# Later sums, a deeper staging ring and an even chain pattern in a transformer block

## The chip, the core and the metric

The kernel runs on one core of a Trainium2 chip. The metric is the device time of one execution in microseconds. Before the change it is 2608.06 us, the median of three runs (2605.62 to 2611.5).

A core has a matrix engine (PE, with its weight loads shown as PEld), a vector engine (DVE), a scalar engine (ACT), GpSimd (POOL) and SyncE (SP). Each runs its instructions strictly in the order in which they were put, and waits where an operand or a buffer is not ready. Here SP only issues DMAs; ACT and POOL issue some too, in their own order of work.

## The reference

```python
x = x + attention(tc_rmsnorm(x, t, g1, b1), Wq, Wk, Wv, Wo)
x = x + swiglu(tc_rmsnorm(x, t, g2, b2), gate_w, hid_w, out_w)
# around it: out = x_in + x
# tc_rmsnorm: g * x * rsqrt(mean(x * x) + 1e-6) + b, with g and b linear in t
# attention:  16 heads of 32, softmax(q k^T / sqrt(32)) v, then Wo
# swiglu:     silu(x @ gate_w.T) * (x @ hid_w.T) @ out_w.T, hidden width 2048
# x: (4, 1024, 512) float32; t: (4, 128)
```

## The kernel before

The 4096 tokens are eight blocks of 512 (two to a batch entry). The heads are taken in groups of four. One **unit of attention** `j` is half a block's queries (256) for one head group; its 1024 keys come in four **slots** of 256 keys. So there are 8 x 4 x 2 x 4 = 256 slots `g`, 32 to a block, and a loop `while g < END` writes out by hand what each engine does in each slot. The order of the instructions on PE, DVE, ACT and POOL is exactly that of the code. SP's DMAs are ordered by the scheduler. `kind = g % 4` is the place of a slot in its **group** of four.

What a slot does:

- `scores(g)` multiplies queries and keys on PE into four PSUM banks (tag `sc`, one tile); `keep(g)` copies them on ACT to an SBUF tile `raw` (a ring of nine); `running_max` takes maxima on DVE, in two instructions.
- In kind 0 `max_T` transposes the maxima of the unit before on PE, `parts` reduces them on DVE, and in kind 1 `parts_T` and `spread` bring them back as `shift`, with copies on ACT.
- Five slots after `scores`, `shifted` subtracts the maximum (DVE) and `exponential` follows (ACT); six slots after, `weighted` multiplies by the values (PE), and `accumulate` adds the slots of one unit in SBUF with an accumulating DMA of 1 MB (POOL).
- The **sums of a unit**: `fold_sum` (DVE) adds the two halves of the accumulated tile, `sums` (PE) adds over partitions into a PSUM tile of tag `w` (two banks), `sums_out` copies it to SBUF (ACT) and writes it to DRAM; `take` reads it back in another layout, `invert` takes the reciprocal (DVE), `put` writes it, and `sums_in` spreads it over partitions; `normalize` applies it. `sums_out`, `take` and `put` issue their DMAs from ACT; `sums_in` from SP. For the last two units `inverse` takes the reciprocal directly.

Slots 0 to 59 are the **opening** (`FS` is 60). There PE also computes the projections of keys, queries and values for all four batch entries. One projection of 512 tokens is a **chain**: PE fills one bank, ACT evicts it (`evict`) to a staging tile of tag `st`, a ring of two, and SP stores it to DRAM (`kqs`, `vs`), from where the attention loads it later. The chains wait in a queue with the slot from which each may run. A credit decides how many run in a slot: it grows by `PACE` = 1.5 per slot, up to 2.9, and each chain that runs takes 1. The first chain of a slot is evicted in the same slot, the second (`late`) early in the next. Chains of the output projection (`project_out`) have their own queue, `first`; when one is `due` it goes ahead.

From slot 60 the **feed-forward** fills PE instead. A pair `p` of slots makes 128 hidden features for one block: `pair_15`, `pair_26`, `pair_7`, `pair_3` and `pair_4` are products that share sums of weights and tokens (tiles `pa` of tag `w`, and `pb`); `take_5`, `add_15`, `copy_156` and `sub_5` combine them on ACT and DVE; `gate_tanh`, `gate` and `hidden` make the feature tile `h` (a ring of seven), which frees `pa` and `pb`. `filler` contracts four finished features with `out_w` (tile `pc`, tag `w`). The kinds 0 and 2 are the even slots of a pair, 1 and 3 the odd ones. `take_5` also uses a tile of tag `st`.

In the profile the lines are: `mm` L106 (all 32-column products), `take` L152, `invert` L157, `put` L162, `spread_inverse` L168, evictions L235 and L248, `scores` L278, `keep` L285, `running_max` L290 and L293, `max_T` L299, `parts` L305 to L310, `parts_T` L315 and L317, `spread` L325 and L326, `shifted` L331, `exponential` L334, `weighted` L344, `accumulate` L358, `fold_sum` L366, `sums` L376, `sums_out` L381 with its DMA at L146, `take_5` L496, `add_15` L500, `copy_156` L515, `sub_5` L522, `gate` L537, `hidden` L540, `take_contract` L553.

Of the kernel before, what the change touches and what calls it, by code (L numbers as in the profile page):

```python
# [10 lines left out]
F32 = mybir.dt.float32  # L11
# [6 lines left out]
P = 128  # L18
NB = 512
# [5 lines left out]
def tile_cond_transformer_block(  # L25
# [133 lines left out]
    def put(tag: str):  # L159
        few = state.pop(("few", tag))  # L160
        inv_s[tag] = tc.dram_tile(list(few.shape), F32, name=f"invs{tag}")
        nc.scalar.dma_start(out=inv_s[tag], in_=few)  # L162
# [55 lines left out]
    def load_wkq(hg: int):  # L218
        t = sb.tile([P, 2, C, P], F32, tag="fw", name=f"wkq{hg}", bufs=4)
        nc.sync.dma_start(out=t, in_=kq_w[hg])  # L220
        wkq[hg] = t


    def project_kq(b: int, hg: int, which: int, half: int):
        pp = bank(f"pkq{b}_{hg}_{which}_{half}")
        for c in range(C):
            mm(pp, wkq[hg][:, which, c, :], y[b, half][:, c, :], c == 0, c == C - 1)

        def evict():
            if (b, hg) == (0, 0) and (which, half) != (1, 1):  # L230
                at = which * L + half * NB
                t = kq[0][:, at : at + NB]
            else:
                t = sb.tile([P, NB], F32, tag="st", name=f"st{b}_{hg}_{which}_{half}", bufs=2)
            nc.scalar.activation(t, pp, AF.Copy, scale=SCALE if which else 1.0)  # L235
            nc.sync.dma_start(out=kq_s[b, hg][:, which, half * NB : (half + 1) * NB], in_=t)

        return evict

    def project_v(b: int, kt: int):  # L240
        half, col = divmod(kt * P, NB)
        pp = bank(f"pv{b}_{kt}")
        for c in range(C):
            mm(pp, y[b, half][:, c, col : col + P], wv[0][:, c, :], c == 0, c == C - 1)

        def evict():
            t = sb.tile([P, NB], F32, tag="st", name=f"sv{b}_{kt}", bufs=2)
            nc.scalar.copy(t, pp)  # L248
            nc.sync.dma_start(out=v_s[b][:, :, kt, :], in_=t.rearrange("p (a c) -> p a c", a=C))

        return evict
# [15 lines left out]
    def scores(r: int):  # L267

        j, u = divmod(r, UN)
        m, qh = divmod(j, NB // HQ)  # L270
        t = kq[m]
        sc = ps_sc.tile([P, HG, 2, HQ], F32, tag="sc", name=f"sc{r}")
        q0 = L + qh * HQ
        for k in range(2):
            kt = 2 * u + k
            for i in range(HG):
                rows = slice(i * DH, (i + 1) * DH)
                nc.tensor.matmul(  # L278
                    sc[:, i, k, :], t[rows, kt * P : (kt + 1) * P], t[rows, q0 : q0 + HQ], start=True, stop=True
                )  # L280
        raw[r] = sb.tile([P, 2, HG, HQ], F32, tag="raw", name=f"raw{r}", bufs=RAW)
        state["sc", r] = sc

    def keep(r: int):
        nc.scalar.copy(raw[r].rearrange("p k h q -> p h k q"), state.pop(("sc", r)))  # L285

    def running_max(r: int, k: int):
# [76 lines left out]
    def fold_sum(j: int):  # L364
        t = acc[j]
        nc.vector.tensor_tensor(t[:, 0, :, :], t[:, 0, :, :], t[:, 1, :, :], ALU.add)  # L366
# [5 lines left out]
    def sums(j: int):  # L372
        total = ps.tile([P, HQ], F32, tag="w", name=f"sum{j}")
        a = acc.pop(j)
        for i in range(HG):
            nc.tensor.matmul(total[i * DH : (i + 1) * DH, :], ones_sum, a[:, 0, i, :], start=True, stop=True)  # L376
        state["sum", j] = total

    def sums_out(j: int):
        t = sb.tile([P, HQ], F32, tag="rec", name=f"total{j}", bufs=2)  # L380
        nc.scalar.copy(t, state.pop(("sum", j)))  # L381
        compact(f"s{j}", t, DH, HQ)
# [6 lines left out]
    def inverse(j: int):  # L389
        rec = sb.tile([P, HQ], F32, tag="rec", name=f"rec{j}", bufs=2)  # L390
        nc.vector.reciprocal(rec, state.pop(("sum", j)))  # L391
        state["rec", j] = rec
# [141 lines left out]
    def gate(p: int):  # L534

        h[p] = sb.tile([P, NB], F32, tag="h", name=f"h{p}", bufs=7)
        nc.vector.scalar_tensor_tensor(h[p], state.pop(("t", p)), 1.0, bank_a.pop(p), ALU.add, ALU.mult)  # L537
# [117 lines left out]
    def chain(g: int, spare: int = 0):  # L655

        q = first if first and first[0][0] <= g else queue
        if not q or (g >= 0 and q[0][0] > g) or (q is queue and len(q) <= spare):
            return None
        _, load, fn, a = q.popleft()  # L660
        if load is not None:
            fetch()
        return fn(*a)

    with tc.manual_schedule(
# [34 lines left out]

        direct = NR // UN - 2
        late = None
        credit = 0.0
        g = 0
        END = NR + 12
        NP_ = NBLK * NF
# [20 lines left out]
        while g < END:  # L727
# [19 lines left out]
                scores(g)  # L747
            if kind == 1 and m_on:
                spread(j_m, 0)
            if kind == 3 and s_on:  # L750
                fold_sum(j_s)
            if kind == 0 and n_on and j_n >= direct:
                inverse(j_n)
            if x_on and kind != 1:
                shifted(r_x)
            if late is not None:
# [5 lines left out]
                normalize(j_o)  # L762
            if kind == 1 and n_on and j_n < direct:
                take(f"s{j_n}")
            if kind == 3 and n_on and j_n < direct:
                put(f"s{j_n}")
            for fn, a in pinned.pop(g, []):
                fn(*a)
            if v_on:
# [6 lines left out]
                shifted(r_x, slice(HG // 2, HG))  # L776
            if g < NR:
                keep(g)
            if kind == 0 and o_on:
                sums_in(j_o)  # L780
            if kind == 1 and s_on:
# [2 lines left out]
            if not ffn:  # L784
                if x_on:
                    exponential(r_x)
                credit = min(credit + PACE, 2.9)
                evict = None
                if credit >= 1 or due or kind == 0:
                    evict = chain(g, FG)  # L790
                    credit -= evict is not None
                if g < NR:
                    running_max(g, 0)
                    running_max(g, 1)
                if evict is not None:
                    evict()
                for fn, a in halfway.pop(g, []):
                    fn(*a)
                if kind == 0 and m_on:
                    columns[0] = P  # L800
                    max_T(j_m)
                    parts(j_m)
                if g == FS - 1:
                    columns[0] = DH
                    pair_15(0)
                    take_5(0)
                    add_15(0)
                elif credit >= 1 or due or kind == 0:
                    late = chain(g, FG)
                    credit -= late is not None  # L810
                if kind == 3 and s_on:
                    sums(j_s)
                    sums_out(j_s)
                if g in (FS - 4, FS - 3):
                    load_f(0, g - FS + 4)
                if g == FS - 1:
                    load_f(1, 0)
            elif even:
                load_f(p + 1, 1)
                pair_26(p)  # L820
                copy_156(p)
                if x_on:
                    exponential(r_x)
                if kind == 0 and m_on:
                    max_T(j_m)
                    parts(j_m)
                one, two, evict = filler(p)
                one()
                two()
                if g < NR:  # L830
                    running_max(g, 0)
                    running_max(g, 1)
                if evict is not None:
                    evict()
                if kind == 0:
                    pair_7(p)
                    sub_5(p)
                for fn, a in halfway.pop(g, []):
                    fn(*a)
            else:  # L840
                load_f(p + 2, 0)
                if due or len(queue) > FG:
                    chain(g)()
                if kind == 3:
                    pair_7(p)
                    sub_5(p)
                pair_3(p)
                if kind == 3:
                    gate_tanh(p)
                if x_on:  # L850
                    exponential(r_x)
                pair_15(p + 1)
                take_5(p + 1)
                if kind == 1:
                    gate_tanh(p)
                if g < NR:
                    running_max(g, 0)
                if kind == 3:
                    gate(p)
                if g < NR:  # L860
                    running_max(g, 1)
                add_15(p + 1)
                if kind == 1:
                    gate(p)
                pair_4(p)
                hidden(p)
                if due:
                    chain(g)()
                if kind == 3 and s_on:
                    sums(j_s)  # L870
                    if j_s < direct:
                        sums_out(j_s)
                for fn, a in halfway.pop(g, []):
                    fn(*a)
            if kind == 2 and n_on and j_n < direct:
# [98 lines left out]
```

## Time and profile before

| what | value |
|---|---|
| median of three runs | 2608.06 us |
| the profiled execution, its own time | 2606.2 us |
| its span | 2604.4 us |
| PE busy | 2434.4 us, 93% of the span |
| DVE busy | 1845.1 us, 71% |
| ACT busy | 1409.4 us, 54% |
| moved by DMA | 510.64 MB, 196 GB/s on average |
| granted PE clock, mean | 0.98 |

A profile line for a group of instructions gives the source line, engine and operation, what is written and read with the shape, how often, the busy time, the mean of one, and the idle time of the engine just before it with what ended most of it. A line of the waits reads "engine, tile and line that waited <- what it waited for: microseconds in total, times, longest". A line of the timeline gives the start, the length, the instruction and, in brackets, how long the engine had been idle and what released it. "pa L106 x16" in a timeline is several instructions of the same kind merged; the start of the next line tells better than the length when the engine could go on, since lengths of matmuls overlap.

### The profile page before, as it was taken

What the parts mean: (1) busy time and instruction counts of PE and PEld (TensorE: products, weight loads), DVE (VectorE), ACT (ScalarE), POOL (GpSimd) and SP (SyncE); (2) the same over time, 40 slices, a digit from 0 to 9 for tenths busy, and PEclk for the clock granted to TensorE, in tenths of its full rate; (3) what the DMA queues carried; (4) which work ended last, traced back from release to release, by engine and by line L of the source; (5) the groups of instructions that cost most, each with busy time, mean ns of one, the idle gap of its engine ahead of it and who ended that gap; (6) DMA issues with size and microseconds to landing.
All of it is one profiled execution on the core that took longest, in us unless ns stands there. A gap on an engine that the chain in (4) does not pass through costs nothing. (4 is left out here: it accounts for less than half of the span.)

```text
span 2604.4 us, 71655 instructions
## 1 busy us (share of the span) xinstructions
PE 2434.4 (93%) x31785; PEld 1134.6 (44%) x31785; DVE 1845.1 (71%) x2180; ACT 1409.4 (54%) x1485; POOL 172.4 (7%) x207
## 2 busy tenths in 40 slices
PE   8899898899999899999999999999999999989999
PEld 3333333334444444444444444444444444434444
DVE  2677676857777888788868886887788778843332
ACT  3566666666556655665655665655566556512110
POOL 0000000000000000000000000000000000000000
PEclk9999999999999999999999999999999999999999
DMA  5698898877887888789878887888788878763442
GB/s 193 178 256 238 222 243 212 225 201 187 209 195 183 209 226 209 175 200 226 209 184 200 217 217 182 202 210 211 189 203 208 211 190 194 188 173 107 136 133 90
DMA packets 216386, 510.64 MB, mean 196 GB/s; under 512 B 43407, under 2 KB 84359, under 8 KB 188686
## 3 DMA queue, kind: packets, MB, share of 16 engines
q0 software_dynamic: 28656, 208.68, 41.5%
q1 hardware_dynamic: 166752, 296.56, 34.8%
q8 instruction: 250, 4.10, 0.6%
q10 hardware_dynamic: 20670, 0.83, 0.6%
q14 instruction: 58, 0.48, 0.1%
HBM read 254.82 MB, written 42.48 MB: 114 GB/s over the span
## 5 line engine op out<-in xcount | busy, mean ns | idle before, releaser
L331 DVE TENSOR_TENSOR raw<-raw,shift 128x2048 f32<-128x2048 f32 (+1 forms) x320 | 595.1, 1860 | 128.6 <-ACT shift L326 123.3
L285 ACT COPY raw<-sc 128x2048 f32<-128x2048 f32 x256 | 479.9, 1875 | 171.8 <-DVE fews L157 63.7
L334 ACT ACTIVATE raw<-raw 128x2048 f32<-128x2048 f32 x256 | 491.2, 1919 | 130.5 <-DVE raw L331 130.3
L290 DVE TENSOR_TENSOR rmax<-rmax,raw 128x1024 f32<-128x1024 f32 x384 | 469.5, 1223 | 67.1 <-ACT raw L285 61.9
L106 PE MATMUL pc<-h,ow 128*32 128x512 f32 x4096 | 468.7, 594 | 0.2 <-DVE rec L391 0.2
L106 PE MATMUL pa<-x,fw 128*32 128x256 f32 x6144 | 383.2, 382 | 6.8 <-DVE pa L500 6.8
L278 PE MATMUL sc<-kq 32*128 32x256 f32 x4096 | 302.3, 410 | 10.1 <-ACT raw L285 10.1
L344 PE MATMUL av<-raw,v 128*32 128x256 f32 x4096 | 282.2, 394 | 18.7 <-ACT raw L334 18.6
L358 POOL DMA_DIRECT2D raw<-raw x192 | 165.3, 861 | 2023.6 <-ACT raw L334 911.8
L106 PE MATMUL pa<-sums,fw 128*32 128x256 f32 x4096 | 269.2, 381 | 0.0
L106 PEld LDWEIGHTS pa<-x,fw 128*32 128x32 f32 x6144 | 194.6, 110 | 159.2 <-issue 24.6
L278 PEld LDWEIGHTS sc<-kq 32*128 32x128 f32 x4096 | 190.1, 189 | 145.8 <-issue 103.4
L106 PE MATMUL pkq<-y,wkq 128*32 128x512 f32 (+1 forms) x1760 | 237.4, 608 | 9.1 <-ACT y L182 4.1
L106 PEld LDWEIGHTS pc<-h,ow 128*32 128x32 f32 x4096 | 128.8, 110 | 244.0 <-issue 218.8
L344 PEld LDWEIGHTS av<-raw,v 128*32 128x32 f32 x4096 | 109.1, 111 | 147.3 <-issue 56.3
L106 PEld LDWEIGHTS pa<-sums,fw 128*32 128x32 f32 x4096 | 133.8, 111 | 88.9 <-issue 1.8
L106 PE MATMUL pb<-sums,fw 128*32 128x256 f32 x2048 | 137.7, 387 | 31.0 <-DVE pb L522 30.4
L305 DVE TENSOR_REDUCE top<-mt 128x8 f32<-128x1024 f32 x64 | 78.3, 1223 | 104.8 <-PE mt L299 104.8
L532 ACT ACTIVATE t<-pa 128x512 f32<-128x512 f32 x128 | 78.1, 610 | 111.9 <-PE pa L106 111.9
L553 DVE SCALAR_TENSOR_TENSOR res<-pc,res 128x512 f32<-128x512 f32 x128 | 88.2, 689 | 70.1 <-PE pc L106 70.1
L106 PE MATMUL pb<-x,fw 128*32 128x256 f32 x2048 | 134.0, 379 | 1.2 <-ACT pb L515 1.2
L106 PEld LDWEIGHTS pkq<-y,wkq 128*32 128x32 f32 (+1 forms) x1760 | 72.3, 118 | 143.6 <-issue 128.3
(100 smaller groups left out, 1894.8 us busy)
## 6 DMA issues: line engine op xcount, KB each, us to landing
raw<-raw POOLq DMA_DIRECT2D x192, 1024.0 KB, 8.8
fw<-sw SPq DMA_DIRECT2D x256, 256.0 KB
ow<-in_out_w SPq DMA_DIRECT2D x128, 256.0 KB
fw<-in_gh_w SPq DMA_DIRECT2D x128, 256.0 KB
wkq<-in_kq_w SPq DMA_DIRECT2D x32, 512.0 KB
v<-vs SPq DMA_DIRECT2D x32, 512.0 KB
fw<-in_gh_w SPq DMA_DIRECT2D x128, 128.0 KB
kq<-kqs SPq DMA_DIRECT2D x31, 512.0 KB
```

The lines of the kernel that those rows point to most:

```text
L106: nc.tensor.matmul(dst[k : k + n, :], w[:, k : k + n], moving, start=start, stop=stop, skip_group_check=seeded)
L278: nc.tensor.matmul(sc[:, i, k, :], t[rows, kt * P : (kt + 1) * P], t[rows, q0 : q0 + HQ], start=True, stop=True)
L285: nc.scalar.copy(raw[r].rearrange("p k h q -> p h k q"), state.pop(("sc", r)))
L290: nc.vector.tensor_tensor(rmax[j], rmax[j], raw[r][:, k, :, :], ALU.max)
L305: nc.vector.tensor_reduce(top, state.pop(("mt", j)), AX.X, ALU.max)
L331: nc.vector.tensor_tensor(t, t, s.unsqueeze(1).to_broadcast(list(t.shape)), ALU.add)
L334: nc.scalar.activation(raw[r], raw[r], AF.Exp)
L344: nc.tensor.matmul(av[j][i * DH : (i + 1) * DH, :], v[m][:, kt, i * DH : (i + 1) * DH], raw[r][:, k, i, :], start=(kt == 0), stop=(kt == K ...
L358: nc.gpsimd.dma_start(out=acc[j].rearrange("p k h q -> p (k h q)"), in_=raw[r].rearrange("p k h q -> p (k h q)"), accum_op=ALU.add,)
L532: nc.scalar.activation(state["t", p], bank_a[p], AF.Tanh, scale=0.5)
L553: nc.vector.scalar_tensor_tensor(r, pp, 0.5, r, ALU.mult, ALU.add)
```

## The change

Four edits:

1. In the opening, staging tiles come from the ring of `h` (seven tiles) instead of `st` (two), through a new helper `staging`. From the moment the sums of tokens exist (end of slot 58) they come from `st` again.
2. The fold of a unit moves from the head of its kind 3 slot to the end of it (opening), or to the place between `add_15` and `hidden` (feed-forward). `sums` moves from the end of that slot to the next slot, kind 0, right behind `scores`; `sums_out` follows `keep` there.
3. `put` moves behind `keep` in its slot, kind 3. The `raw` tile of a slot is allocated in `keep` instead of `scores`.
4. The credit goes. In the opening every slot runs one chain, and every even slot a second: two, one, two and one in a group.

```diff
+    def staging(name: str):
+        if "sums" in state:
+            return sb.tile([P, NB], F32, tag="st", name=name, bufs=2)
+        return sb.tile([P, NB], F32, tag="h", name=name, bufs=7)
...
-                t = sb.tile([P, NB], F32, tag="st", name=f"st{b}_{hg}_{which}_{half}", bufs=2)
+                t = staging(f"st{b}_{hg}_{which}_{half}")
...
-            t = sb.tile([P, NB], F32, tag="st", name=f"sv{b}_{kt}", bufs=2)
+            t = staging(f"sv{b}_{kt}")
...
-        raw[r] = sb.tile([P, 2, HG, HQ], F32, tag="raw", name=f"raw{r}", bufs=RAW)
         state["sc", r] = sc
     def keep(r: int):
+        raw[r] = sb.tile([P, 2, HG, HQ], F32, tag="raw", name=f"raw{r}", bufs=RAW)
...
             if kind == 1 and m_on:
                 spread(j_m, 0)
-            if kind == 3 and s_on:
-                fold_sum(j_s)
-            if kind == 0 and n_on and j_n >= direct:
-                inverse(j_n)
+            if kind == 0 and n_on:
+                sums(j_n)
+                if j_n >= direct:
+                    inverse(j_n)
...
-            if kind == 3 and n_on and j_n < direct:
-                put(f"s{j_n}")
...
             if g < NR:
                 keep(g)
+            if kind == 0 and n_on and j_n < direct:
+                sums_out(j_n)
+            if kind == 3 and n_on and j_n < direct:
+                put(f"s{j_n}")
...
-                credit = min(credit + PACE, 2.9)
-                evict = None
-                if credit >= 1 or due or kind == 0:
-                    evict = chain(g, FG)
-                    credit -= evict is not None
+                evict = chain(g, FG)
...
-                elif credit >= 1 or due or kind == 0:
+                elif even:
                     late = chain(g, FG)
-                    credit -= late is not None
                 if kind == 3 and s_on:
-                    sums(j_s)
-                    sums_out(j_s)
+                    fold_sum(j_s)
...
                 if kind == 1:
                     gate(p)
+                if kind == 3 and s_on:
+                    fold_sum(j_s)
                 pair_4(p)
                 hidden(p)
...
-                if kind == 3 and s_on:
-                    sums(j_s)
-                    if j_s < direct:
-                        sums_out(j_s)
```

## The prediction

> **What bounds the kernel now.** I read the page's busy table first, then the stretches by 100 us, then the waits of PE, ACT and DVE in two windows (opening 0 to 620 us, feed-forward 620 to 2380), then the timelines of single slots.
>
> ```profile
> PE 2434.4 (93%) x31785; PEld 1134.6 (44%) x31785; DVE 1845.1 (71%) x2180; ACT 1409.4 (54%) x1485; POOL 172.4 (7%) x207
> 300.00:400.00 100.00, 87.69 (x844) 33.40 (x843) 67.27 (x73) 61.91 (x65) 6.88 (x8) 0.92 0.85 239
> 700.00:800.00 100.00, 96.93 (x1346) 45.73 (x1342) 76.40 (x92) 53.98 (x56) 7.74 (x9) 1.00 0.81 194
> ```
>
> PE bounds, so what counts is PE's idle time and its slowed time. In the stretches (columns: length, then PE, PEld, DVE, ACT, POOL busy, clock, DMA share) the opening is the poor part: PE 88% busy at clock 0.92, against 97% at 1.00 later.
>
> ```profile
> ACT st L235 <- DMA kqs<-st: 46.3, 9, 8.4
> 345.17 0.60 ACT L235 ACTIVATE st<-pkq 128x512 f32<-128x512 f32 x1 [7.61 <-DMA kqs<-st]
> 347.46 0.58 PE L325 MATMUL sp<-mT,select 12*128 12x256 bf16 x2 [1.89 <-ACT mT L317]
> 347.97 1.94 PE L344 MATMUL av<-raw,v 128*32 128x256 f32 x16
> ```
>
> First line, ACT's waits in the opening: an eviction of a projection waits for the store of an earlier one, which holds one of two `st` buffers. The others show one case: ACT stands 7.61 us, the copy of `mT` behind it is late, PE idles 1.89 us, and then 16 matmuls that take 1.07 us elsewhere take 1.94, at a lower clock.
>
> ```profile
> PE sum L376 <- DVE h L537: 23.0, 38, 0.7
> PE pb L106 <- DVE pb L522: 30.4, 10, 4.8
> ACT raw L285 <- DVE fews L157: 61.2, 31, 2.0
> 994.16 1.05 PE L106 MATMUL pb<-sums,fw 128*32 128x256 f32 x16
> 995.79 0.64 PE L376 MATMUL sum<-raw,ones_sum 128*32 128x256 f32 x8 [0.58 <-DVE h L537]
> 996.36 1.15 PE L278 MATMUL sc<-kq 32*128 32x256 f32 x16
> 990.30 1.17 DVE L366 TENSOR_TENSOR raw<-raw 128x1024 f32<-128x1024 f32 x1
> 995.06 0.68 DVE L537 SCALAR_TENSOR_TENSOR h<-t,pa 128x512 f32<-128x512 f32 x1
> 995.66 1.22 DVE L290 TENSOR_TENSOR rmax<-rmax,raw 128x1024 f32<-128x1024 f32 x1
> 996.79 0.43 DVE L500 TENSOR_TENSOR pa<-pa,p 128x256 f32<-128x256 f32 x1
> ```
>
> These are waits in the feed-forward, then the end of a kind 3 slot. `sums` waits for a PSUM bank that `gate` (L537) frees. DVE has no gap in this slot, from the fold (L366) to the end: its order, not its load over the whole, sets the moment.
>
> **What the Trainium skill says.** "TensorE: Matmul & The Clock Gate", "What's actually happening": an idle array falls to half clock and needs a busy window of about 3.4 us to recover. The slowing agrees (1.94 against 1.07 us); the page's idle window of 3.4 us doesn't, waits of 2.3 us suffice here. "Perfetto Trace Analysis", "Optimization Strategy": a bubble that repeats can mean too few buffers. Agrees: nine waits on `st`. "DMA: Bandwidth & Descriptors", "Anatomy of one DMA — SWDGE (gpsimd) path": a semaphore wait ahead of a DMA is made by the issuing sequencer. Agrees: `keep` (L285) stands up to 2.0 us behind `put`, whose reciprocal is late.
>
> **The change, part by part.** Sums are against this execution: 2606.2 us, span 2604.4; the median of the runs shown, 2608.06, is 1.9 above.
>
> *Staging in the `h` ring (seven).* From PE's timeline, slot 0 starts at 49.7 us and slot 60 at 592.5. Eight groups of four slots, 186.0 to 477.7, take 36.46 each. PE's own work in one, by start to start: six chains of 3.55 (333.82 to 337.37), four scores 1.08, four weighted 0.89, sums 0.55, transposes 0.92, parts and spreads 0.85: 31.5. The excess of 5.0 is 3.1 idle (24.9 in the eight) and 1.5 of clock (windows of 20 us: 0.59 of a window lost). Of the 24.9, I trace to ACT stalls on stores: 1.89 at 347; 2.33 and 2.50 after 313.9; 2.61 and 0.66 after 392.8; 1.84 after 236.4; 0.91 after 244.6: 12.7. With 2.0 at 124 and 2.6 at 567 it is 17. Clock lost in the windows with such stalls is 0.77 of 20 us, 15; half of it, 8, I put to them, since DVE's waits lie there too. Together 25. Six chains come in 36 us, so seven buffers last about 40 us against a store's 7.4 (issued 337.80, released 345.17): no wait remains. Late next is `parts` on DVE, which keeps PE 2.33 us at five places whatever ACT does; I give back 4. **Gain 21.**
>
> *Two, one, two, one.* The credit gave 2,2,1,2 and 2,1,1,1 by turns; the chains are as many (four left at slot 60 both times), so PE's work is equal. With no second chain ahead of `sums`, a wait like the 4.16 us at 591.5 (bank held by the last eviction) goes, and ACT no longer holds `keep` for `total` (17.0 us in eight waits, mostly free). 9 us, bounds 0 and 15. Loads in SP's queue swap places with a few stores here; at a DMA share of 0.85 I count nothing, bounds of 5 either way. POOL's order is unchanged.
>
> *Fold and sums.* Nothing is removed. Normal group, with the case above: the fold leaves the slot's head, so `shifted`, `sub_5`, the maxima and `gate` end 1.1 earlier; the fold follows `add_15` and ends at 995.66 - 1.09 + (1.13 + 0.33 + 1.09) = 997.1. PE ends `pair_4` at 995.1, runs scores to 996.2, **waits 0.95 us for the fold**, sums to 997.75, where `weighted` starts; before it started at 997.44. With semaphores +0.4 us. `hidden` ends as before; behind PE's wait stand `weighted` and all of the next slot. Some 30 groups: +12. In six groups with two output projections in the slot, the wait of 0.81 for `x` goes: -5. In six with a norm, where sub_5 keeps PE 3.30 us and sums and scores run at half clock (2.1 and 1.0 us), `weighted` can start near 1143.1 instead of 1144.1: -6. In three, fold waits for a transfer (12.1 us in four waits, to 5.9) and pb loses 1.6 to 2.3; the fold now comes later: -6. The last two groups take their inverse in the slot of the sums: 1 us either way. **Net -5**, bounds -15 and +15. In the opening the fold behind the maxima costs 0 to 0.8 in 14 groups: +5.
>
> *Moved DMAs, all on ACT's queue.* `put` behind `keep`: 1.4 us later, and SP's first spread load with it (990.41 to 997.90 now, 7.5 us; SP waits there 94.1 us in all). Behind it on SP stand weight loads that are used over 13 us later, and the spread rows are used at 1017: nothing. `sums_out` behind `keep`: issued near 998.5 to 1000 instead of 996.9, while `take` reads it at 1007.3. The gap falls from 10.4 to 8 or 9. One landing shows indirectly: 1206.35 to 1207.90. So nothing; if it took as long as `put`'s 7.5 to 9, ACT and PE lose up to 0.8 in 48 groups. Raw tiles allocated in `keep` take the same buffers as built: nothing either way.
>
> Sum: -21 - 9 + 5 - 5 = -30: 2576 for the profiled execution, **2578** as a median.
>
> **Rivals.** *The next limit takes it (chance 0.14).* With ACT free, DMA (share 0.85 to 0.93 in the opening) and DVE's `parts` catch PE: staging gives 5, pattern 0, fold costs 5, feed-forward as above: about 2603. For it: 2.33 us waits on `parts` repeat. Against: 12.7 of 24.9 us of idle follow store stalls. *The stores still hold ACT* (the change doesn't do what it says) gives the same. *The fold becomes the bound (0.09), slower.* In kind 0, PE waits for a fold behind `add_15`, itself behind ACT's copy `p` and a 1.9 us exponential. At 0.4 us a normal group it costs 12; 1.0 us more, 1.4, eats the whole gain of 30, and 1.9 gives 2608 + 15 = 2623. For: DVE is dense there. Against: `p` is copied by 995.9, before `add_15` wants it. *Full floor*: the opening near 32.5 a group, 2550; inside the first forecast's tail.
>
> **Numbers.** Forecast 0.77. 0.2% is 5.2 us, about what a measurement of this kernel can tell: faster below 2602.8. Nearly all of the forecast (0.76) and half of the next-limit case (0.07) make 0.83; the other half is same, 0.07; the fold's case and a rest of 0.01 are slower, 0.10. The range 2555 to 2606 takes in opening gains from about 0 to 50 and leaves out the fold's case and the floor.
>
> **What would show it.** Right: no `st` wait on `kqs` above 1 us; slots 0 to 60 in about 518 us instead of 542.8; opening clock above 0.96; PE's wait at L376 <- DVE fold, about 1 us in 30 groups, in place of `h`; normal group 30.9 instead of 30.5 us; no `keep` behind `fews`. Wrong: ACT waiting at `take` for `sumss`; opening groups still over 35.5 us with DVE or DMA as releaser; fold waits over 1.4 us.

## The result and the profile after

The changed kernel takes **2618.15 us** (median of 12 runs, 2609.97 to 2625.4) against 2609.78 of the kernel before in the same session (12 runs): a ratio of **1.0031, 95% interval 1.0015 to 1.0047**. It is 8 us slower, where 30 faster was forecast. The profiled execution has a span of 2618.8 us and a time of 2620.56.

The stretches of the kernel after, columns as before (length, busy PE, PEld, DVE, ACT, POOL, clock, DMA share):

```profile
300.00:400.00 100.00, 94.94 (x950) 38.24 (x953) 77.09 (x83) 71.14 (x74) 7.67 (x9) 0.98 0.96 263
700.00:800.00 100.00, 96.91 (x1352) 47.12 (x1344) 78.06 (x91) 58.28 (x61) 7.75 (x9) 1.00 0.80 188
```

The stretch that was poor is mended: PE 95% busy at clock 0.98, where it had 88% at 0.92. The loss must lie elsewhere. From PE's timeline, by the starts of slots 0, 60 and 252:

| | slots 0 to 60 | slots 60 to 252 |
|---|---|---|
| before | 542.8 us | 1640.7 us |
| after | 527.2 (-15.6) | 1667.9 (+27.2) |

The waits of the kernel after, of ACT over the whole run and of PE in the feed-forward (total us, times, longest):

```profile
ACT shift L332 <- DMA rec<-invss: 39.9, 10, 5.0
ACT raw L291 <- DMA raw<-raw: 81.0, 35, 5.9
PE pa L106 <- ACT shift L332: 30.0, 11, 3.9
PE sum L382 <- issue: 27.9, 14, 7.5
PE sum L382 <- PE sc L284: 21.7, 23, 1.0
```

Lines 1 and 3 are new: in the kernel before no `shift` copy waits longer than 0.73 us for a DMA. ACT's copy of `shift` (L332) waits ten times for a DMA that has nothing to do with it, and PE behind it. Lines 4 and 5 are PE waiting at `sums`, in both for the fold, though the releaser named is another: in the trace the fold ends 0.1 us ahead of `sums` each time, and both lines are gone in the experiments that put the fold first. The second line stands where `keep` waited for `fews` before (63.7 us in the whole run, now 11.7): with `put` gone from ahead of it, `keep` waits longer for the accumulating DMA that frees its `raw` buffer (81.0 us against 46.6 before).

The timeline of the kernel after, group 100:

```profile
931.05 5.30 SPq L168 DMA_DIRECT2D rec<-invss  x4
...
938.35 0.58 ACT L332 COPY shift<-sp 128x512 f32<-128x512 f32 x1 [0.92 <-PE sp L331]
...
942.76 0.32 ACTq L152 DMA_DIRECT2D fews<-sumss  x1
...
943.13 0.58 ACT L332 COPY shift<-sp 128x512 f32<-128x512 f32 x1 [4.19 <-DMA rec<-invss]
...
943.76 1.93 PE L106 MATMUL pa<-x,fw 128*32 128x256 f32 x16 [3.13 <-ACT shift L332]
```

Between ACT's two `shift` copies stands the `take` (L152). The first copy ends at 938.93; the DMA of `take` goes out only at 942.76. The second copy, whose product PE has had ready since 939.6, starts behind it. PE loses 3.13 us and then runs 16 matmuls in 1.93 us instead of 1.07. The slot takes 10.8 us instead of 6.2.

The same place in the kernel before:

```profile
943.70 0.59 ACT L326 COPY shift<-sp 128x512 f32<-128x512 f32 x1 [0.92 <-PE sp L325]
943.76 0.35 ACTq L152 DMA_DIRECT2D fews<-sumss  x1
945.02 0.59 ACT L326 COPY shift<-sp 128x512 f32<-128x512 f32 x1 [0.73 <-DMA rec<-invss]
```

Here `take` goes out at once, and the 0.73 us are the idle time that nearly every feed-forward slot of this kind has at this place, whatever releaser is named.

Why does `take` wait for `rec`, the spread of another unit's inverse, on another queue? In the built program the DMAs of ACT and SP signal their completion on eight semaphores, handed out in turn. Before a DMA goes out on one of them, the issuing engine waits for the earlier DMA on the same one, where it hasn't done so yet. For unit 22 it reads:

```
          own semaphore   waits for, ahead of the issue of take 22
before    3               3: sumss22 (ACT)   2: invss20 (ACT)
after     3               4: sumss22 (ACT)   3: rec21 (SP)
```

Before, `take` of this unit shared its semaphore with the write that it reads back anyway. The change puts the DMAs into another order, so the turn comes out otherwise, and here `take` shares with the first of the four DMAs of `rec21`. SP issues them from 931.05 to 936.35, and `take` goes at 942.76, when that first one has landed.

Sharing alone costs nothing. By the semaphores that the traces mark, 32 of the 50 `take`s of the feed-forward (units 12 to 61) share with a `rec` in the changed kernel, and 25 in the kernel before. ACT is held in eleven of these, all in the changed kernel: units 19, 22, 27, 30 and so on (`j % 8` is 3 or 6, from 19 to 59; the profile names `rec` in ten of them). There ACT comes to `take` 5.1 to 9.3 us after the issue of `rec`, which lands 8.7 to 12.5 us after it. In the other 21 it lands 1.7 to 8.7 us after its issue, ahead of `take`.

The Trainium skill, "DMA: Bandwidth & Descriptors", "Why a DMA increments its semaphore by 16 and not by 1", says that with two DMAs in flight on one semaphore a wait for the earlier one's count can pass before it has landed. That is a reason for such a wait; what the runs show is the wait. "Perfetto Trace Analysis", "DMA Instruction — HWDGE (DVE, Sync)", puts the wait ahead of the start that the profiler reports. That agrees: the issue shows 0.32 us, and the wait appears only as idle time of the next instruction.

The second new wait, group 92 of the kernel after:

```profile
861.08 0.35 ACT L502 COPY p<-pa 128x256 f32<-128x256 f32 x1
...
862.34 0.43 DVE L506 TENSOR_TENSOR pa<-pa,p 128x256 f32<-128x256 f32 x1
...
862.67 1.22 DVE L372 TENSOR_TENSOR raw<-raw 128x1024 f32<-128x1024 f32 x1
...
863.99 1.08 PE L382 MATMUL sum<-raw,ones_sum 128*32 128x256 f32 x8 [1.65 <-issue]
...
864.82 1.97 PE L350 MATMUL av<-raw,v 128*32 128x256 f32 x16
```

The fold (L372) stands behind `add_15` (L506), and that behind ACT's copy `p` (L502). It ends at 863.89 and `sums` starts 0.1 later: the releaser is the fold, though the row says "issue". Besides 1.65 us of idle, the sums and `weighted` take 1.08 and 1.97 us at the lower clock, where 0.64 and 1.07 are usual.

### The profile page after: what moved, and what is told of

Its sections match the earlier page's. It is cut to its first block, busy times and chain, and to the rows that moved or that the text cites. A ratio compares the mean times of both kernels' runs of the same rounds, so it can differ in the third digit from the quotient of the medians.

```text
span 2618.8 us, 71682 instructions
## 1 busy us (share of the span) xinstructions
PE 2435.8 (93%) x31785; PEld 1162.2 (44%) x31785; DVE 1846.6 (71%) x2180; ACT 1406.9 (54%) x1485; POOL 172.4 (7%) x207
## 5 line engine op out<-in xcount | busy, mean ns | idle before, releaser
L106 PE MATMUL pa<-x,fw 128*32 128x256 f32 x6144 | 394.1, 387 | 30.2 <-ACT shift L332 30.0
L106 PEld LDWEIGHTS pa<-x,fw 128*32 128x32 f32 x6144 | 201.2, 111 | 182.7 <-ACT shift L332 40.5
L106 PE MATMUL pa<-sums,fw 128*32 128x256 f32 x4096 | 276.7, 388 | 0.0
L106 PE MATMUL pkq<-y,wkq 128*32 128x512 f32 (+1 forms) x1664 | 238.3, 607 | 10.2 <-DMA wkq<-in_kq_w 6.0
L106 PEld LDWEIGHTS pa<-sums,fw 128*32 128x32 f32 x4096 | 141.2, 113 | 88.3 <-issue 8.8
L350 PEld LDWEIGHTS av<-raw,v 128*32 128x32 f32 x4096 | 120.8, 111 | 121.8 <-issue 39.2
L332 ACT COPY shift<-sp 128x512 f32<-128x512 f32 x128 | 75.0, 586 | 145.1 <-PE sp L331 96.6
L521 ACT COPY pb<-pa 128x256 f32<-128x256 f32 x128 | 45.8, 358 | 194.8 <-PE pa L106 178.8
```

Source lines behind the costliest of these rows:

```text
L106: nc.tensor.matmul(dst[k : k + n, :], w[:, k : k + n], moving, start=start, stop=stop, skip_group_check=seeded)
L332: nc.scalar.copy(shift[j][:, k : k + 2, :], pp)
L350: nc.tensor.matmul(av[j][i * DH : (i + 1) * DH, :], v[m][:, kt, i * DH : (i + 1) * DH], raw[r][:, k, i, :], start=(kt == 0), stop=(kt == K ...
```

## The experiments

Theory A: `take` on ACT, held by a shared semaphore, costs the feed-forward. Theory B: the later place of `sums_out` makes the data late. Beside them: the place of the fold on DVE, and whether staging and pattern do what was forecast. The kernels have 4 to 14 runs each. Ratios are to the kernel before in the same session. Its medians were 2609.1 to 2615.0 from session to session, so experiments of different sessions are better compared by ratios than by medians. Opening and feed-forward come from one profiled execution each; it lay 10 us under the kernel's median in experiment 1, and 10 and 13 us over it in 4 and 6.

| kernel | ratio (95% interval) | median us | opening | feed-forward |
|---|---|---|---|---|
| after | 1.0031 (1.0015 to 1.0047) | 2618.2 | 527.2 | 1667.9 |
| 1 after, write of sums in two | 0.9992 (0.9976 to 1.0007) | 2607.9 | 530.7 | 1642.8 |
| 2 staging alone | 0.9915 (0.9900 to 0.9930) | 2585.4 | 517.4 | 1643.2 |
| 3 pattern alone | 0.9953 (0.9936 to 0.9970) | 2595.1 | 529.2 | 1643.4 |
| 4 fold, sums, put alone | 1.0083 (1.0062 to 1.0105) | 2629.2 | 541.2 | 1668.8 |
| 5 staging and pattern | 0.9864 (0.9844 to 0.9884) | 2578.2 | 509.6 | 1645.6 |
| 6 staging and sums | 0.9938 (0.9919 to 0.9957) | 2599.0 | 523.3 | 1659.1 |
| 7 after, take by SP | 0.9861 (0.9839 to 0.9883) | 2579.4 | 510.4 | 1641.3 |
| 8 as 1, fold first | 0.9912 (0.9892 to 0.9932) | 2591.9 | 513.2 | 1648.9 |
| 9 before, write of sums in two | 1.0190 (1.0171 to 1.0209) | 2659.4 | 551.9 | 1683.6 |
| 10 as 5, take by SP | 0.9871 (0.9852 to 0.9889) | 2574.8 | 508.9 | 1638.4 |
| 11 after, fold first, take by SP | 0.9793 (0.9777 to 0.9808) | 2556.3 | 495.9 | 1629.3 |
| 12 as 11, put ahead of keep | 0.9775 (0.9753 to 0.9798) | 2549.3 | 497.7 | 1626.1 |
| 13 after, fold first | 0.9874 (0.9856 to 0.9892) | 2576.6 | 504.0 | 1638.2 |

### 1: the write of the sums in two DMAs

One more DMA per unit moves the turn of the semaphores, and `take` no longer shares with a late `rec`.

```diff
-        nc.scalar.dma_start(out=inv_s[tag], in_=t[0:P:rows, :])
+        for at in range(0, n, n // 2):
+            nc.scalar.dma_start(out=inv_s[tag][:, at : at + n // 2], in_=t[0:P:rows, at : at + n // 2])
```

> The changed kernel, with the write of a unit's sums (sums_out) issued as two DMAs of half the columns instead of one. The order of all work stays; only the DMAs' completion semaphores, eight that the scheduler hands out in turn, fall differently: the take of units 19, 22, 27, 30, ... (remainder 3 or 6 by 8) no longer shares one with a spread of the reciprocals issued by SP just before. Theory A (take waits on ACT for that other DMA's completion, not for its data): ACT's waits before the second shift copy on 'rec<-invss' (39.9 us in 10) vanish, the kind 1 slots of about 11 us in these groups return to 6.2, and the time falls by 30 to 46 us, to about 2578. Theory B (take waits for the landing of the sums, whose gap to take the change cut from 10.4 to about 8 us): the waits stay or grow, since two DMAs are issued later than one; the time stays at 2618 or rises by up to 20.

The wait of `shift` for `rec` is gone from ACT's waits, PE's wait for `shift` is down to 0.6 us in two, and the feed-forward falls by 25.1 us. Waits of PE in this kernel (lines are one higher):

```profile
PE sum L383 <- issue: 41.6, 19, 7.4
PE sum L383 <- PE sc L285: 20.4, 21, 1.0
PE pa L106 <- ACT shift L333: 0.6, 2, 0.4
```

The waits for the fold stay. The median falls by only 10 us, in part because the profiled execution lies under it, in part because the second write has prices of its own. In many units the pair shows 1.8 us on ACT where the one write shows 0.50; what lengthens it isn't shown.

```profile
902.52 1.82 ACTq L147 DMA_DIRECT2D sumss<-total  x2
```

And the turn that frees `take` holds another DMA. By the semaphores in the trace the second write is held on its own semaphore eight times, 3.2 to 8.0 us, 38.1 us in all: six times behind a load of `kq`, three times in the opening, which gains nothing.

### 2, 3 and 4: each part alone

All on the kernel before. Experiment 2:

```diff
-                t = sb.tile([P, NB], F32, tag="st", name=f"st{b}_{hg}_{which}_{half}", bufs=2)
+                t = staging(f"st{b}_{hg}_{which}_{half}")
...
-            t = sb.tile([P, NB], F32, tag="st", name=f"sv{b}_{kt}", bufs=2)
+            t = staging(f"sv{b}_{kt}")
```

> The kernel before, with staging tiles from the ring of h alone. Theory A of the opening (waits on stores were worth their 21 us): slots 0 to 60 in about 522 us instead of 542.9, time about 2588. Rival (the pattern made the opening's gain): slots 0 to 60 above 537 us, time within 5 us of before. The feed-forward from slot 60 keeps its 1641 us under both.

Experiment 3:

```diff
-                credit = min(credit + PACE, 2.9)
-                evict = None
-                if credit >= 1 or due or kind == 0:
-                    evict = chain(g, FG)
-                    credit -= evict is not None
+                evict = chain(g, FG)
...
-                elif credit >= 1 or due or kind == 0:
+                elif even:
                     late = chain(g, FG)
-                    credit -= late is not None
```

> The kernel before, with two, one, two and one chain in place of the credit, two staging buffers. If the pattern is worth 0 to 9 us as predicted: slots 0 to 60 in 534 to 543 us. Rival (the pattern is what gained): about 527 us. Possible too: with two staging buffers the second chain in kind 2 runs into stores as before, and nothing changes.

Experiment 4, staging tiles left in `st` and the credit as before (the feed-forward's hunks and those of `put` and `raw` are as in the change):

```diff
-            if kind == 3 and s_on:
-                fold_sum(j_s)
+            if kind == 0 and n_on:
+                sums(j_n)
...
+            if kind == 0 and n_on and j_n < direct:
+                sums_out(j_n)
...
-                    sums(j_s)
-                    sums_out(j_s)
+                    fold_sum(j_s)
```

> The kernel before, with fold, sums, sums_out, put and the allocation of raw moved as in the change, staging and credit as before. Theory A (these moves carry the whole loss, by way of take): feed-forward from slot 60 to 252 about 1668 us instead of 1641, with ACT's waits on 'rec<-invss' of about 40 us; opening 540 to 548; time about 2635. Rival (the feed-forward lost through the opening's other state, such as loads that arrive later): about 1641 us, time about 2610.

Staging takes 25.4 us out of the opening, just what the working had before it gave 4 back (22 by the ratio). The pattern alone takes 13.6, with waits on `kqs` of 34.7 us still there. The moves alone have nearly the whole loss of the feed-forward, +28.1 against the changed kernel's +27.2 (in an execution 10 us over its median), and take 1.6 from the opening. But the three don't add up: the changed kernel's opening is 10 us worse than with staging alone.

### 5 and 6: which pair spoils the opening

On the kernel before, experiment 5 makes the edits of 2 and 3; experiment 6 those of 2, 4 and 1. The lines that name each:

```diff
+                t = staging(f"st{b}_{hg}_{which}_{half}")
...
+                evict = chain(g, FG)
```

```diff
+                t = staging(f"st{b}_{hg}_{which}_{half}")
...
+        for at in range(0, n, n // 2):
...
+                sums(j_n)
```

> The kernel before with staging in the ring of the feed-forward and with the pattern of two, one, two and one chain, without the moves of fold and sums. Alone the two took 25.4 and 13.6 us from the opening of 542.8; the changed kernel, with all three, has 527.2. If the two parts help different slots: opening 504 to 508, feed-forward as before (1641 to 1645), median about 2571. If both gain by ending the same waits (ACT held by st behind kqs, which lowers PE's clock), the opening stays at 515 to 519 and the median at 2582 to 2587. If the pattern spoils the staging by asking for chains faster than their weights and stores land, the opening is 525 to 530 as in the changed kernel, and the median 2592 to 2597.

> The kernel before with the staging and with the moves of fold and sums, the write of the sums' results cut into two DMAs as in the first experiment (so that take shares no completion semaphore with a late spread), the pattern by credit as before. If the moves of sums are what costs the opening of the changed kernel its 10 us against staging alone: opening 524 to 530, and the median, with a feed-forward of 1643, is 2592 to 2598. If they are harmless there and the pattern is at fault: opening 514 to 519, median 2582 to 2588. In both, no wait of ACT's shift copy on rec<-invss in the feed-forward.

Staging and pattern together give 509.6, 33.2 less than before: the forecast's 25 and 9 nearly to the microsecond, and the pattern spoils nothing. So it is the moves that cost the opening: the changed kernel has them besides, and is at 527.2. Experiment 6 doesn't show this by itself. Its 523.3 is worse than staging alone, but its second write of the sums is held in the opening four times, 15.6 us in all, and the profiled execution was its slowest; its feed-forward isn't used.

### 7: take by SP

```diff
-        nc.scalar.dma_start(out=few, in_=src.rearrange("h (p c) -> (h p) c", c=few.shape[1]))
+        nc.sync.dma_start(out=few, in_=src.rearrange("h (p c) -> (h p) c", c=few.shape[1]))
```

> The changed kernel with the DMA of take issued by SP in place of ACT, so that a completion semaphore that comes late can hold only SP's queue. Theory of the shared semaphore on ACT: PE's waits for the shift copy (pa <- ACT shift, 30 us in 11 slots) go, the slots of kind 1 in groups 88, 100, 120, 132 and so on fall from 10.7 to 12.5 us to 6.2, and the feed-forward from 1667.9 to 1640 to 1650 us, unless SP's queue, held at take, makes fews late and with it sum_in (then PE or DVE waits for fews appear and the gain is half or less: 1652 to 1665). Theory of the late data of sumss: take on SP waits for the same data, so the chain behind fews moves by nothing and the feed-forward stays within 3 us of 1668.

This is 39 us less than the changed kernel by the medians and 44 by the ratios; by profile 26.6 in the feed-forward and 16.8 in the opening, which I had not foreseen. In the opening of the changed kernel ACT's `shift` copies wait three times for a DMA, 6.1 us together, for other loads and stores; with `take` by SP never. That is less than 16.8, and the rest isn't traced. The timeline at the same place of group 100:

```profile
914.80 5.12 SPq L168 DMA_DIRECT2D rec<-invss  x4
...
921.80 0.59 ACT L332 COPY shift<-sp 128x512 f32<-128x512 f32 x1 [0.91 <-PE sp L331]
...
923.12 0.59 ACT L332 COPY shift<-sp 128x512 f32<-128x512 f32 x1 [0.73 <-PE sp L331]
...
925.54 0.34 SPq L152 DMA_DIRECT2D fews<-sumss  x1
```

`take` still goes out 2.4 us after the second copy has begun, but it holds SP's queue, not ACT, and nobody needs `fews` so soon. SP's queue now waits for `sumss` 133.5 us in all, at no visible cost to PE.

### 8: fold first, on top of 1

```diff
+            if kind == 3 and s_on:
+                fold_sum(j_s)
             if kind == 0 and n_on:
                 sums(j_n)
...
-                if kind == 3 and s_on:
-                    fold_sum(j_s)
```

(Both later places of the fold go.)

> The kernel of the first experiment (the changed kernel with the write of the sums' results in two DMAs), with the fold of a group put back at the head of DVE's slot of kind 3, the sums staying in the slot of kind 0. If PE's wait for the fold is a true cost (21.7 us in 23 groups, and 27.9 in 14 shown as issue): these lines fall under 3 us, normal groups go from 30.3 to 30.8 to about 29.5 us, the feed-forward from 1642.8 to 1615 to 1625 and the median by 15 to 25 us. If DVE's work ahead of the parts is the rival cost (the fold at the head holds running_max and the parts of the same slot by its 1.5 us), other waits of PE take its place and the feed-forward stays at 1638 to 1647.

All waits of PE at `sums` for the fold are gone, and normal groups take 29.8 us instead of 30.3; the median falls by 16 (21 by the ratios). By profile, though, the gain is in the opening (530.7 to 513.2), and the feed-forward is 6 us longer: groups 88 and 184 took 42 us instead of 36 and 37. There the second write of the sums is held again behind a load of `kq`, for 7.9 and 7.5 us where the first experiment has 3.6 and 4.0. In group 88:

```profile
808.49 8.86 ACTq L147 DMA_DIRECT2D sumss<-total  x2
817.45 0.36 ACT L522 COPY pb<-pa 128x256 f32<-128x256 f32 x1 [8.99 <-DMA kq<-kqs]
817.86 1.82 PE L106 MATMUL pb<-x,fw 128*32 128x256 f32 x16 [4.95 <-ACT pb L522]
```

These two groups are 11.6 us longer than in the first experiment, more than the 6 that the feed-forward grew by. So the longer feed-forward doesn't speak against putting the fold first.

### 9: the first experiment's edit on the kernel before

```diff
-        nc.scalar.dma_start(out=inv_s[tag], in_=t[0:P:rows, :])
+        for at in range(0, n, n // 2):
+            nc.scalar.dma_start(out=inv_s[tag][:, at : at + n // 2], in_=t[0:P:rows, at : at + n // 2])
```

> The kernel before, none of the change made, with the one edit of the first experiment: the write of the sums' results goes out in two DMAs of half the size. With the rotation of completion semaphores moved by one DMA a group, the takes of units 19, 22, 27, 30 and so on now share theirs with the spread rec of the unit before, as they do in the changed kernel and did not in the kernel before. Theory of the shared semaphore: ACT waits about 4 us at the shift copies behind these eleven takes (shift <- DMA rec<-invss near 40 us), the slots of kind 1 in groups 88, 100, 120, 132, 152, 164, 184, 196, 216, 228 go from 6.2 to 10 to 12 us, and the feed-forward from 1640.7 to 1658 to 1670 us; the median is 15 to 40 us above before's. Theory that the later place of sums_out in the changed kernel costs the time: sums_out lies here where it was, so the feed-forward stays at 1638 to 1645 and the median within 6 us of before's.

The same edit that speeds the changed kernel by 10 us slows the kernel before by 50. The turn of the semaphores is the other way round here: `take` of unit 22 now waits for `rec21`. Waits of this kernel, ACT's and PE's:

```profile
ACT shift L327 <- DMA rec<-invss: 29.0, 8, 4.4
ACT shift L327 <- DMA fw<-in_gh_w: 8.5, 2, 4.8
PE pa L106 <- ACT shift L327: 26.9, 10, 3.7
ACT raw L286 <- DMA sumss<-total: 30.0, 21, 2.2
```

The first two rows are the ten `take`s in units 19 to 54, 37.5 us; the second row names a load, but by the built program these two wait for `rec37` and `rec45` as well. `sums_out` lies where it always lay, so theory B falls. The feed-forward grew by 43 us, where 17 to 29 were expected. The groups of these ten `take`s grew by 31.7 together. The rest fits the second write, which was in no theory: `keep` (L286) waits for it 30.0 us in 21 (5.2 in three before), and PE at `max_T` for `keep` 24.6 us in the feed-forward instead of 9.9.

### 10 and 11: without the moves, and with the fold first, take by SP in both

The line of experiment 7, in 10 on the kernel of experiment 5, in 11 on the changed kernel together with the fold's lines of experiment 8:

```diff
-        nc.scalar.dma_start(out=few, in_=src.rearrange("h (p c) -> (h p) c", c=few.shape[1]))
+        nc.sync.dma_start(out=few, in_=src.rearrange("h (p c) -> (h p) c", c=few.shape[1]))
...
+            if kind == 3 and s_on:
+                fold_sum(j_s)
```

> The kernel with staging and pattern but without the moves of fold and sums (2578.2 us in the fifth experiment: opening 509.6, feed-forward 1645.6), with the DMA of take issued by SP. If the 39 us that the same edit took from the changed kernel were the shared semaphores, there is little to take here: the long waits behind take are three, 6.6 us, all in the opening; median 2570 to 2580, feed-forward 1640 to 1648. If ACT gains by issuing fewer DMAs in general, 62 issues of some tenths of a us each in the slots of kind 1, the feed-forward falls to 1620 to 1632 and the median to 2550 to 2565. If SP's queue, full of transfers, holds the takes: over 1650 and over 2584.

> The changed kernel with take on SP (2579.4 us in the seventh experiment: opening 510.4, feed-forward 1641.3) and with the fold back at the head of the slot of kind 3, sums still in that of kind 0. If PE's wait for the late fold (19.7 us in 20 groups and 45.6 in 20 shown as issue) is a cost of its own: normal groups 30.3 to 29.8, norm groups 37.7 to 36.6, groups 68, 104, 136, 168 and 200 from 34 to 40 down to 31 to 37, against 39.5 to 40.6 in the groups of po; together 8 to 20 us off, median 2560 to 2572. If the fold's place only trades one wait for another, as the eighth experiment's feed-forward of 1648.9 against 1642.8 has it: feed-forward 1640 to 1650, median 2576 to 2588.

Without the moves, `take` by SP changes nothing that can be told (0.9871 against 0.9864). Its worth in the changed kernel is thus the semaphore, not one issue less on ACT. With the fold first and sums in kind 0, the kernel is at 2556.3, 23 us under experiment 7; more than the best that was expected, 14.5 us of them in the opening. In the feed-forward the groups of a norm go from 37.7 to 36.6 and the normal ones from 30.3 to 29.8, while those of two output projections give back 39.5 to 40.6. Groups 100, 132, 164, 196 and 228 grow too, by 11.4 us together: in each of them the fold, now early, waits for the accumulating DMA of its own unit. The row of DVE in the feed-forward of 11, which neither 7 nor 13 has:

```profile
DVE raw L372 <- DMA raw<-raw: 10.7, 5, 3.2
```

Experiments 10 and 11 differ in the moves of sums, `put` and `raw` with the fold left in place: 1638.4 to 1629.3 and 508.9 to 495.9. So moving `sums` one slot later is good, and moving the fold back with it is not. (The place of `put` is worth nothing that can be told, by experiment 12; the allocation of `raw` had no run of its own.)

### 12 and 13: put back, and the fold first with take still on ACT

For 12, experiment 11 with this; for 13, the changed kernel with the edit of experiment 8 alone:

```diff
+            if kind == 3 and n_on and j_n < direct:
+                put(f"s{j_n}")
             for fn, a in pinned.pop(g, []):
                 fn(*a)
...
-            if kind == 3 and n_on and j_n < direct:
-                put(f"s{j_n}")
```

> The kernel of the eleventh experiment (take by SP, fold first: 2556.3 us, 0.9793 of before; opening 495.9, feed-forward 1629.3) with the put back ahead of keep in the slot of kind 3, where the kernel before has it. If keep's wait behind put was a cost of its own: ACT's keep waits for fews again (63.7 us in the kernel before), raw<-raw falls from 87.5 us towards 47, and the feed-forward rises by 10 to 25 us, median 2566 to 2582. If the two waits take each other's place (raw<-raw down by about what fews brings) and keep isn't on PE's path: feed-forward within 5 us of 1629, median 2551 to 2561. If put's earlier place frees SP's spread and few's buffer earlier: 5 to 10 us faster.

> The changed kernel with one edit: fold back at the head of the slot of kind 3; take stays on ACT, and its semaphore is still that of the late spread. If the late fold costs by itself what it costs with take on SP (2579.4 to 2556.3): 23 us off 2618, median 2590 to 2600, opening 510 to 516, feed-forward 1652 to 1662 with shift <- rec<-invss still at 35 to 42 us. If the two losses lie beside each other (PE held by take where it would wait for the fold anyway): under 10 us off, 2608 to 2620. The prediction's own price for the later fold, 0.4 us in 30 groups and 5 us in the opening less 17 from earlier sums and po groups, would give 2613 to 2623.

12: `keep` waits for `fews` 62.9 us again and for `raw<-raw` 82.4, where it had 11.7 and 87.5. The time doesn't rise, and the intervals of 11 and 12 overlap: `put`'s place costs nothing that PE feels. It is also the fastest kernel of the study, 2.2% under the kernel before.

13: more than any theory gave. The fold first takes 41.5 us off the changed kernel by the medians, 23.2 in the opening and 29.7 in the feed-forward by profile, with the waits at `take` as they were:

```profile
ACT shift L332 <- DMA rec<-invss: 43.1, 12, 5.3
PE pa L106 <- ACT shift L332: 30.7, 11, 4.2
```

Group 92 falls from 33.9 to 31.1, groups 124 and 220 from 33.9 and 33.7 to 30.2 and 29.7. The two losses are not independent. The fold's place costs 18 us where `take` is by SP (7 against 11: 0.0068 of 2609.8) and 41 where it is on ACT (after against 13: 0.0157). The waits at `take` have the same length in both kernels, but the traces show most of the reason. In five of the groups that `take` holds (100, 132, 164, 196, 228) the accumulating DMA has landed by the time of the early fold, so that the fold doesn't wait, and fold first makes these groups 4.1 us shorter; with `take` by SP it makes them 11.4 longer. These 15.5 us are most of the 18 by which the gains in the feed-forward differ (29.7 against 12.0). The opening's difference, 23.2 against 14.5, stays open.

## Why the prediction was wrong

In us against the kernel before (ratios times 2609.8), starting with experiment 5: staging and pattern -35; the moves with the fold left first and `take` out of the way -19 (5 to 11, or -20 from 10); the fold behind `add_15` +18 (11 to 7); `take` on ACT +44 (7 to after). The sum is +8. `take` and the fold could be put on in the other order: `take` +21 first (11 to 13), the fold +41 after. Experiment 7, the change with a `take` that holds no engine that computes, lies at -36: close to the forecast of -30, though its parts are not those of the working, as the fold and the opening show below.

- **Staging, -21, and pattern, -9: right.** Together -33.2 in the opening of experiment 5. Staging alone is 25.4 in the opening and 22 by the ratio, so whether the 4 given back for `parts` on DVE were lost can't be told. So close a match is partly luck: half of the lost clock was put to the stores by assumption, and of the 5.0 us of excess in a group the working names 3.1 and 1.5. One sign came true, no `st` wait on `kqs`; the opening's clock is 0.96 where above 0.96 was named, and slots 0 to 60 took 527.2 us instead of 518, by what the moves cost there.
- **"Moved DMAs ... nothing": the step that failed.** It asked when the data of `put` and `sums_out` would land, and for these it was right: `put`'s place costs nothing, and no `take` is seen waiting long for `sumss` in the feed-forward. It did not ask what else `take` waits for. The step's own words "on ACT's queue" hold the point: whatever holds a DMA's issue holds all of ACT behind it. The passage of the Trainium skill that the prediction took up ("DMA: Bandwidth & Descriptors", "Anatomy of one DMA — SWDGE (gpsimd) path"), that a semaphore wait happens on the issuing sequencer, was applied to `put` alone; the held `take`, up to 4.6 us on ACT, agrees with it. The outer bound, 0.8 us in 48 groups, is 38 us, close to what came, but by another cause, and it wasn't carried into the range.
- **The fold, +12 in normal groups and +5 in the opening: the place was right, the size not.** The 0.4 us of a normal group is 0.5 (30.3 against 29.8), with a wait of 0.5 us at `sums`; PE's wait of 1.0 us stands in 17 other groups. Missed were the groups in which `add_15` itself is late: PE waits there 1.1 to 7.5 us (27.9 in 14). That is the rival "the fold becomes the bound", given 0.09, by its very chain of fold, `add_15`, copy `p`; it was priced as equal in all groups and held off by one slot in which `p` was early. With the opening it comes to 18 us with `take` by SP, near the 17, but as 12.0 in the feed-forward and 14.5 in the opening by profile instead of 12 and 5; with `take` on ACT, as in the change, to 41.
- **Sums earlier against fold later, -17 in the groups with projections, norms and transfers:** those with two projections gained 1.8 each instead of 0.8 (41.3 to 39.5). The groups with a norm had 37.6 before and 37.7 after: nothing instead of 1, since the fold was behind the norm's work; fold first, they gain 1.0. The three groups in which the fold waits for a transfer (100, 132 and 196) take 30.8 us each in experiment 7 against 32.4, 32.9 and 33.5 before: 6.4 less, as forecast. In the changed kernel they take 35.6, 35.6 and 37.7, since `take` is held in just these.
- **"Normal group 30.9 instead of 30.5"** read: 30.3 in the changed kernel, against 30.6 before in the same groups. **"No keep behind fews"**: right (63.7 to 11.7), and worth nothing, since `raw<-raw` took its place.

"Wrong" was to show as ACT waiting at `take` for `sumss`; it showed at `take`, for something else. It was also to show as fold waits over 1.4 us, and these came: up to 7.5.

## What to carry to other kernels

When a change moves the order of DMAs, list for every DMA on a computing engine's queue which completion semaphore it uses and who had that one before; an issue can wait for an unrelated transfer of another engine, and it shows in the profile only as idle time of the next instruction, put down to that transfer. Look at how long that transfer takes to land, since sharing alone costs nothing, and at all the DMAs: the edit that freed `take` in experiment 1 held the second write instead. Give DMAs that may wait to an engine that computes nothing. And price an instruction that goes behind others by the groups in which those others are late, not by a quiet one.

## What the runs showed of the hardware

Cutting one small write into two DMAs, with the same bytes in all, took 1.8 us of ACT in many units instead of 0.50, and more where the second one was held: 8.9 us in group 88 of experiment 8. The four issues of one spread (`rec`) took SP 2.0 us in group 92 and 5.3 in group 100, and the `take` that waits for the first of these four went out 11.7 us after that one was issued.

In group 92 of the changed kernel the lower clock came with a delay: behind PE's wait of 2.13 us for `pb`, 16 matmuls still took 1.07 us, and only the scores after them 1.71 instead of 1.15. PE need not be idle throughout for this. The clock record of this kernel grants half the clock 25 times from slot 0 on, for 3.4 to 10.2 us; in the 3.4 us ahead of each time PE had been busy between 0 and 51% by the profile. This fits that waits of 1.7 to 3.1 us, shorter than the window that the prediction quotes, were enough.
